# Attention over full 64-row tiles, with a short path chosen by a bound of all scores, and two key chunks per group

## The chip, the cores and the metric

The kernel runs on one core of one Trainium2 chip. A core has a matrix engine (TensorE, PE in the profile, with its weight loads shown as PEld), a vector engine (VectorE, DVE), a scalar engine (ScalarE, ACT), a general engine (GpSimd, POOL) and an engine that only issues transfers here (SyncE, SP). The metric is the time of one execution on the device in microseconds, from the first instruction to the last. Lower is better.

## The reference

The kernel computes one transformer block with adaptive layer norm, on x of shape (2, 2048, 576), with 16 heads of 36 features, everything in 32-bit floats. Cut to what matters:

```python
mod = silu(c) @ w_ada + b_ada                # six vectors of 576 per image
xn  = ln(x, 1e-6) * (1 + sc_msa) + sh_msa
q, k, v = split(xn @ w_qkv + b_qkv)          # (2, 2048, 16, 36) each
q = ln(q, 1e-5, qn_g, qn_b)                  # per head, over its 36 features
k = ln(k, 1e-5, kn_g, kn_b)
attn = softmax(einsum('bqhd,bkhd->bhqk', q, k) * 36 ** -0.5)
o = einsum('bhqk,bkhd->bqhd', attn, v) @ w_proj + b_proj
x = x + g_msa * o
h = gelu(modulated_ln(x) @ w1 + b1)          # 576 -> 2304
return x + g_mlp * (h @ w2 + b2)
```

In the inputs the gains qn_g and kn_g are ones, and the biases qn_b and kn_b are zeros.

## The kernel before

The work runs in stages: the modulation vectors (lines 121 to 181); then for each of the two images the attention inputs (L220), attention (L289) and the projection (L423); then the feed-forward part over blocks of 512 rows (L468 on). A framework turns the program into one instruction list for each engine. It keeps the written order as a priority, but an instruction that isn't ready can be passed by later ones. An engine executes its list in order, and waits where an operand or a buffer isn't there. SyncE's list holds nearly all loads, in the written order; the loads of the attention weights (L225 to L227) are written after the modulation stage and don't depend on it.

Attention works on pairs of heads. A pair's two heads of 36 features are padded to 64 rows each, so that one fills partitions 0 to 63 and the other 64 to 127. `prepare` takes one block of 512 rows of q or k: GpSimd copies it into a padded `stage` tile whose remaining rows are zero, four TensorE transposes turn it by features into the one bank `tp`, and VectorE moves it into `kt` or `qt` with gain and bias. Eight such blocks make a pair (four of k, four of q).

The softmax needs two rounds. In the first, `largest` multiplies q by k with one tile of 128 queries against 512 keys, for both heads, on 36 rows each (L338), and VectorE takes the largest score of each query (L345). `shifted_q` then puts the negated maximum into the 37th feature of a fresh copy of q (the `stage_m` tiles), against a row of ones in k, so that the second round gives shifted scores. In the second round `scores` takes a chunk of 128 keys against a block of 512 queries, on 37 rows (L360), and ScalarE applies the exponential (L364). `values` multiplies the result by v on all 128 rows, with 64 output columns for each head (L370), and accumulates over the 16 key chunks in the one bank `acc`. A 37th column of ones in v gives the sum of the softmax. `finish` copies `acc` to SBUF on ScalarE (L380), transposes it back (L383), and VectorE divides (L386, L388).

The loop at L402 goes over 8 pairs and 64 steps (4 query blocks of 16 key chunks). A step issues the scores of one chunk, a max step of the next pair, and the values of the chunk before. The first pair's max round stands alone ahead of the loop (L398), and the last pair has no max round beside it. Every matmul in 32-bit floats is two instructions. PSUM holds three double banks for scores and maxima (`s`), one `acc` and one `tp`.

## Time and profile before

| | |
|---|---|
| median of 3 runs | 6044.8 us (6020.16 to 6089.19) |
| the profiled execution | 6044.47 us |
| its span | 6042.7 us, 47052 instructions |
| mean granted TensorE clock | 0.878 of full speed |
| TensorE busy | 5862.5 us (97%) |
| VectorE, ScalarE, GpSimd busy | 1873.6, 1441.3, 288.1 us |
| chain of work that ended last | scores L360 21%, values L370 20%, max round L338 19%, feed-forward L507 10%, attention inputs L244 9% |

The profile is one execution on the chip. The clock is the share of full speed that the chip granted to TensorE; the profile gives it for each of 40 slices, or for any stretch. A busy time of TensorE is the time in which at least one matmul was under way, so two that run side by side count once. A group row gives the line, engine, operation and operands, the count, the busy time, the mean of one in ns, and the idle time before them with what ended it. A timeline row gives the start and the length in us of neighbouring instructions of one kind; the distance from one start to the next shows what a part really costs, since the ends are modelled.

### The profile page before, as it was taken

Reading aid. Unit: us, or ns where it says so; the run is one execution under the profiler, and the core shown is the slowest. Engines: PE = TensorE matmul, PEld = TensorE weight load, DVE = VectorE, ACT = ScalarE, POOL = GpSimd, SP = SyncE. Lnnn points to the kernel's source line nnn. Section 1 sums busy time; section 2 is a strip of 40 time slices with the busy share of each in tenths; the row PEclk is TensorE's granted clock in tenths of the full one; section 3 lists DMA queues with packets and bytes.
Section 4 is the critical chain, followed back from the end, with each engine's and each line's share of the span. In section 5 each row is a group of like instructions: output and inputs, shape, how many; then the busy total and the mean of one; then the engine's idle time right before and its main releaser. Section 6 shows DMA issues by size and latency. Waiting matters only on the chain.

```text
span 6042.7 us, 47052 instructions
## 1 busy us (share of the span) xinstructions
PE 5862.5 (97%) x20336; PEld 2405.9 (40%) x20336; DVE 1873.6 (31%) x2128; ACT 1441.3 (24%) x1789; POOL 288.1 (5%) x388
## 2 busy tenths in 40 slices
PE   8999999999999998999999999999999699999999
PEld 5643323332323325653233323233223355555555
DVE  3453433443433312445343334334321100000000
ACT  1101322332322342110232323223233111111110
POOL 0110000000000002110000000000001100000000
PEclk9965977997978899985898879779799899999999
DMA  3000000000000004000000000000001300000000
GB/s 107 10 1 0 1 1 0 0 1 1 1 0 1 1 1 128 12 0 0 0 1 0 1 0 0 0 0 1 0 1 50 119 16 16 16 16 16 16 8 8
DMA packets 35392, 83.60 MB, mean 14 GB/s; under 512 B 4832, under 2 KB 4832, under 8 KB 35184
## 3 DMA queue, kind: packets, MB, share of 16 engines
q1 hardware_dynamic: 29936, 61.69, 3.3%
q0 software_dynamic: 5248, 18.90, 0.8%
q8 instruction: 159, 2.61, 0.2%
q14 instruction: 49, 0.40, 0.0%
HBM read 61.68 MB, written 18.89 MB: 13 GB/s over the span
## 4 chain that ended last, share of the span: by engine, by line
PE 92%; issue 4%; DMA 1%; DVE 1%; SPq 0%; POOL 0%; ACT 0%; POOLq 0%; DVEq 0%; ACTq 0%
PE s L360 21%; PE acc L370 20%; PE s L338 19%; PE s L507 10%; PE s L244 9%; PE s L521 7%; PE s L445 3%; PE tp L313 2%; PE tp L204 1%; PE tp L383 1%; PE tp L133 0%; DMA x<-x_dram 0%; DVE qs L316 0%; DMA xt<-in_x_dram 0%; DMA wa<-in_w_ada_dram 0%
## 5 line engine op out<-in xcount | busy, mean ns | idle before, releaser
L345 DVE TENSOR_REDUCE mx<-s 128x2 f32<-128x1024 f32 x1024 | 1255.7, 1226 | 1987.9 <-PE s L338 1987.9
L364 ACT ACTIVATE pt<-s 128x1024 f32<-128x1024 f32 x1024 | 1047.7, 1023 | 2299.6 <-PE s L360 2299.5
L360 PE MATMUL s<-qs,kt 37*128 37x512 f32 x4096 | 1332.6, 732 | 14.5 <-DVE qs L316 14.5
L338 PE MATMUL s<-kt,qt 36*128 36x512 f32 x4096 | 1310.4, 735 | 0.0
L370 PE MATMUL acc<-pt,vt 128*64 128x512 f32 x4096 | 1274.6, 705 | 0.7 <-ACT pt L364 0.7
L338 PEld LDWEIGHTS s<-kt,qt 36*128 36x128 f32 x4096 | 489.2, 232 | 651.2 <-issue 648.9
L360 PEld LDWEIGHTS s<-qs,kt 37*128 37x128 f32 x4096 | 349.6, 208 | 893.5 <-issue 559.8
L507 PE MATMUL s<-xnt,w_sb 128*128 128x512 f32 (+1 forms) x1440 | 676.5, 614 | 0.3 <-ACT xnt L212 0.3
L370 PEld LDWEIGHTS acc<-pt,vt 128*64 128x64 f32 x4096 | 221.6, 148 | 878.6 <-issue 868.7
L521 PE MATMUL s<-w_sb,ht 128*128 128x288 f32 x2304 | 563.9, 407 | 0.0
L244 PE MATMUL s<-wq,xnt 128*128 128x288 f32 (+1 forms) x1920 | 542.8, 427 | 8.1 <-DMA wq<-in_w_qkv_dram 7.7
L521 PEld LDWEIGHTS s<-w_sb,ht 128*128 128x128 f32 x2304 | 436.6, 191 | 118.1 <-issue 1.5
L244 PEld LDWEIGHTS s<-wq,xnt 128*128 128x128 f32 (+1 forms) x1920 | 334.9, 190 | 206.2 <-issue 143.0
L507 PEld LDWEIGHTS s<-xnt,w_sb 128*128 128x128 f32 (+1 forms) x1440 | 248.1, 189 | 420.3 <-issue 387.0
L514 ACT ACTIVATE ht<-s,b_sb 128x512 f32<-128x512 f32 x144 | 98.9, 687 | 949.6 <-PE s L507 949.4
L529 DVE TENSOR_TENSOR y<-s,gate 128x576 f32<-128x576 f32 x32 | 24.2, 758 | 604.5 <-PE s L521 604.5
L445 PE MATMUL s<-wp,ott 128*128 128x288 f32 (+1 forms) x640 | 181.3, 426 | 2.2 <-DMA wp<-in_w_proj_dram 2.2
L197 DVE TENSOR_SCALAR xn<-x,mv,rstd 128x576 f32<-128x576 f32 x32 | 18.6, 585 | 491.6 <-PE acc L205 491.1
L308 POOL COPY stage_m<-qk 128x288 f32<-128x288 f32 x64 | 27.2, 427 | 2740.0 <-PE tp L313 2740.0
L445 PEld LDWEIGHTS s<-wp,ott 128*128 128x128 f32 (+1 forms) x640 | 112.1, 191 | 62.5 <-issue 39.6
L316 DVE TENSOR_SCALAR qs<-tp,gain_q,bias_q 128x512 f32<-128x512 f32 x64 | 51.8, 810 | 238.4 <-PE tp L313 238.4
L272 ACT ACTIVATE sq<-qk 128x1152 f32<-128x1152 f32 x32 | 37.2, 1162 | 326.5 <-DVE qk L268 326.5
(84 smaller groups left out, 1636.1 us busy)
## 6 DMA issues: line engine op xcount, KB each, us to landing
xt<-in_x_dram SPq DMA_DIRECT2D x64, 288.0 KB
x_dram<-x POOLq DMA_DIRECT2D x32, 288.0 KB, 3.5
x<-x_dram SPq DMA_DIRECT2D x8, 1152.0 KB
out_dram<-y POOLq DMA_DIRECT2D x32, 288.0 KB, 2.4
wa<-in_w_ada_dram SPq DMA_DIRECT2D x6, 1152.0 KB
wq<-in_w_qkv_dram SPq DMA_DIRECT2D x6, 1152.0 KB
w_sb<-in_w_dram SPq DMA_DIRECT2D x3, 1728.0 KB
w_sb<-in_w_dram SPq DMA_DIRECT2D x4, 1152.0 KB
```

The lines of the kernel that those rows point to most:

```text
L204: nc.tensor.transpose(t4[:, k * P : (k + 1) * P], src[:, k * P : (k + 1) * P], ident)
L244: nc.tensor.matmul(ps[:, a, :HALF], xnt[:kk, k, :], wq[:kk, k, f0 : f0 + HALF], start=(k == 0), stop=(k == NKC - 1),)
L313: nc.tensor.transpose(tp[:, i * P : (i + 1) * P], st[:, i].rearrange("p h e -> p (h e)"), ident)
L338: nc.tensor.matmul(ps[:, h, :], qts[p, blk][r, i * P : (i + 1) * P], kts[p][r, kq * BLK : (kq + 1) * BLK], start=True, stop=True,)
L345: nc.vector.tensor_reduce(maxima[p, blk][:, i, :, kq], ps, AX.X, ALU.max)
L360: nc.tensor.matmul(ps[:, h, :], kts[p][r, kc * P : (kc + 1) * P], qt[r, :], start=True, stop=True)
L364: nc.scalar.activation(pt, ps, AF.Exp, scale=SCALE)
L370: nc.tensor.matmul(acc[64 * h : 64 * h + 64, :], vt[:, v0 : v0 + 64], pt[:, h, :], start=(kc == 0), stop=(kc == NT - 1),)
L445: nc.tensor.matmul(ps[:, a, :HALF], ott[:kk, k, :], wp[:kk, k, a * HALF : (a + 1) * HALF], start=(k == 0), stop=(k == NKC - 1),)
L507: nc.tensor.matmul(ps[:, j, :], w1_sb[:kk, k, f * P : (f + 1) * P], xnt[:kk, k, :], start=(k == 0), stop=(k == NKC - 1),)
L514: nc.scalar.activation(ht[:, f, :], ps[:, j, :], AF.Gelu, bias=b1_sb[:, f : f + 1])
L521: nc.tensor.matmul(ps[:, a, :HALF], ht[:, f, i * P : (i + 1) * P], w2_sb[:, f, a * HALF : (a + 1) * HALF], start=(f == 0), stop=(f == NF - 1),
```

## The change

The kernel now computes a bound on all scores before the stages: after the norm, a head's q and k have at most the length that the largest gain and the largest bias allow. If the bound is at most 32, a flag is 1. All engines read the flag after the modulation stage and branch: on 1, every image's attention takes the new `attention_of_small`, on 0 the old `attention`. Attention inputs, projection and the feed-forward part stand in both branches, unchanged. The PSUM pools are opened once for the modulation stage and again in each branch.

`attention_of_small` has no max round and no shifted q, and applies the exponential to the plain scores. Scores use all 64 rows of a head's tile, of which 28 are zero. A group covers two key chunks: scores of both, then possibly the finish of a query block and a prepare of the next pair, then the values of the group before. Groups run on across pairs without a drain. The copy of `acc` is on VectorE, and the transposes of `finish` come one group later. There are four `pt` buffers instead of three, and k and q of a pair are one tile each. The old path's matmuls of both rounds are also set to 64 rows.

```diff
+    gb = const.tile([1, 2, 2, HD], F32, name="gb")
+    for i, (g_in, b_in) in enumerate(((qn_g, qn_b), (kn_g, kn_b))):
+        nc.scalar.dma_start(out=gb[:, i, 0, :], in_=g_in.unsqueeze(0))
+        nc.scalar.dma_start(out=gb[:, i, 1, :], in_=b_in.unsqueeze(0))
+    neg = const.tile([1, 2, 2, HD], F32, name="neg")
+    nc.vector.tensor_scalar_mul(neg, gb, -1.0)
+    nc.vector.tensor_tensor(neg, neg, gb, ALU.max)
+    most = const.tile([1, 2, 2], F32, name="most")
+    nc.vector.tensor_reduce(most, neg, AX.X, ALU.max)
+    length = const.tile([1, 2], F32, name="length")
+    nc.vector.tensor_reduce(length, most, AX.X, ALU.add)
+    product = const.tile([1, 1], F32, name="product")
+    nc.vector.tensor_tensor(product, length[:, 0:1], length[:, 1:2], ALU.mult)
+    small_sb = const.tile([1, 1], I32, name="small_sb")
+    nc.vector.tensor_scalar(small_sb, product, BOUND / (HD * SCALE), None, ALU.is_le)
...
+    def attention_of_small(b, qk, vt):
...
+            def scores(p, qb, kc):
+                ps = s_tile()
+                for h in range(2):
+                    r = slice(64 * h, 64 * h + 64)
+                    nc.tensor.matmul(
+                        ps[:, h, :],
+                        kts[p][r, kc * P : (kc + 1) * P],
+                        qts[p][r, qb * BLK : (qb + 1) * BLK],
+                        start=True,
+                        stop=True,
+                    )
+                pt = b2p.tile([P, 2, BLK], F32, name="pt", bufs=4)
+                nc.scalar.activation(pt, ps, AF.Exp, scale=SCALE)
+                return pt
...
+            for i in range(2 * NBLK):
+                prepare(0, i)
+            groups = [(p, qb, kc) for p in range(NPAIR) for qb in range(NBLK) for kc in range(0, NT, 2)]
+            per_pair = NBLK * NT // 2
+            behind, done = None, None
+            for g, (p, qb, kc) in enumerate([*groups, (None, None, None)]):
+                pts = None if p is None else [scores(p, qb, kc), scores(p, qb, kc + 1)]
+                if done is not None:
+                    finish(*done)
+                    done = None
+                i, at = divmod(g % per_pair, 3)
+                if p is not None and p + 1 < NPAIR and at == 2 and i < 2 * NBLK:
+                    prepare(p + 1, i)
+                if behind is not None:
+                    bp, bqb, bkc, bpts = behind
+                    if bkc == 0:
+                        acc = acc_tile()
+                    for i in range(2):
+                        values(bp, acc, bpts[i], bkc + i)
+                    if bkc == NT - 2:
+                        ot = b2p.tile([P, BLK], F32, name="ot")
+                        nc.vector.tensor_copy(ot, acc)
+                        done = (bp, bqb, ot)
+                behind = (p, qb, kc, pts)
+            finish(*done)
...
     def attention(b, qk, vt):
...
-                    r = slice(64 * h, 64 * h + HD)
+                    r = slice(64 * h, 64 * h + 64)
...
-                    r = slice(64 * h, 64 * h + HV)
+                    r = slice(64 * h, 64 * h + 64)
...
+    def block(small):
+        with tc.tile_pool(name="qkv", bufs=1) as qkvp:
+            for b in range(B):
...
+                attention_inputs(b, qk, vt, vv)
+                (attention_of_small if small else attention)(b, qk, vt)
+                projection(b, qk)
...
+    is_small = nc.values_load(small_sb[0:1, 0:1], min_val=0, max_val=1)
+    with tc.If(is_small > 0) as branch:
+        with psum_pools():
+            block(True)
+    with branch.Else():
+        with psum_pools():
+            block(False)
```

`prepare`, `values` and `finish` of the new function are those of the old one, but for the tiles and the copy named above.

## The prediction

> **What bounds the kernel now.** I read the groups of instructions first, then stretches with their granted clock, then single steps on the timeline. In the group rows the columns are busy time, mean ns of one, and idle time before.

> ```profile
> PE 5862.5 (97%) x20336; PEld 2405.9 (40%) x20336; DVE 1873.6 (31%) x2128; ACT 1441.3 (24%) x1789; POOL 288.1 (5%) x388
> ...
> PEclk9965977997978899985898879779799899999999
> ```

> ```profile
> L360 PE MATMUL s<-qs,kt 37*128 37x512 f32 x4096 | 1332.6, 732 | 14.5 <-DVE qs L316 14.5
> L338 PE MATMUL s<-kt,qt 36*128 36x512 f32 x4096 | 1310.4, 735 | 0.0
> L370 PE MATMUL acc<-pt,vt 128*64 128x512 f32 x4096 | 1274.6, 705 | 0.7 <-ACT pt L364 0.7
> L345 DVE TENSOR_REDUCE mx<-s 128x2 f32<-128x1024 f32 x1024 | 1255.7, 1226 | 1987.9 <-PE s L338 1987.9
> L364 ACT ACTIVATE pt<-s 128x1024 f32<-128x1024 f32 x1024 | 1047.7, 1023 | 2299.6 <-PE s L360 2299.5
> ...
> L380 ACT COPY ot<-acc 128x512 f32<-128x512 f32 x64 | 37.5, 585 | 176.1 <-PE acc L370 176.1
> ```

> TensorE is busy for 97% of the span; VectorE (L345) and ScalarE (L364) wait for it. Three groups of equal size fill attention: scores (L360), the max round (L338), values (L370). The clock row falls in attention, the middle of each half. The next rows are stretches: start and end, length, PE busy with its instructions, granted clock.

> ```profile
> 382.00:486.00 104.00, 104.00 (x246) 0.50 0.00 0
> ...
> 2160.00:2280.00 120.00, 120.00 (x476) 1.00 0.00 1
> ```

> ```profile
> 362.64:2286.16 1923.52, 1891.05 (x6652) 0.83 0.00 1
> 2692.00:4620.69 1928.69, 1896.50 (x6653) 0.82 0.00 1
> ```

> The first is the max round alone (L338): PE is never idle, yet at half clock throughout. The second is the last head pair, which has no max round: full clock. The last two rows are the attention of image 0 and of image 1, from the first transpose to the last. With a clock of either 0.5 or 1, a mean of 0.83 puts 34% of image 0's time at half clock, and 0.82 puts 36% of image 1's there.

> Single steps (one key chunk: scores, max, values, four matmuls each) show both speeds. First a step at full clock, then one at half, then the end of a half-clock spell:

> ```profile
> 2138.47 1.13 PE L360 MATMUL s<-qs,kt 37*128 37x512 f32 x4
> 2139.43 1.03 PE L338 MATMUL s<-kt,qt 36*128 36x512 f32 x4
> 2140.38 1.08 PE L370 MATMUL acc<-pt,vt 128*64 128x512 f32 x4
> 2141.39 1.13 PE L360 MATMUL s<-qs,kt 37*128 37x512 f32 x4
> ```

> ```profile
> 1002.24 2.08 PE L360 MATMUL s<-qs,kt 37*128 37x512 f32 x4
> 1004.11 1.92 PE L338 MATMUL s<-kt,qt 36*128 36x512 f32 x4
> 1005.96 1.98 PE L370 MATMUL acc<-pt,vt 128*64 128x512 f32 x4
> ```

> ```profile
> 832.04 1.98 PE L370 MATMUL acc<-pt,vt 128*64 128x512 f32 x4
> 833.95 1.12 PE L313 MATMUL tp<-ident,stage_m 128*128 128x128 f32 x4
> 835.00 1.90 PE L370 MATMUL acc<-pt,vt 128*64 128x512 f32 x4
> 836.82 1.13 PE L360 MATMUL s<-qs,kt 37*128 37x512 f32 x4
> ```

> A full-clock step takes 2141.39 - 2138.47 = 2.92 us (0.96 scores, 0.95 max, 1.01 values). At half clock the scores take 1.87 and the max 1.85, the values 833.95 - 832.04 = 1.91: 5.63. The last block shows how a spell ends: values, transposes and values, all on 128 rows, run for 4.8 us without a 36- or 37-row matmul between, and the scores after them take 1.13 again. My reading: the gate opens on a few us in which most array rows work; matmuls on 36 or 37 rows, two at a time, leave it shut, but do not shut it once open if values stand between them.

> [...]

> **The change, part by part, as a new attention stage.** I build it from TensorE's rows, since nothing else is near: per group of two chunks ScalarE has 2 x 1.02 = 2.05 us of exponentials.

> ```profile
> 4606.27 1.13 PE L360 MATMUL s<-qs,kt 37*128 37x512 f32 x4
> 4607.33 1.08 PE L370 MATMUL acc<-pt,vt 128*64 128x512 f32 x4
> 4608.34 1.13 PE L360 MATMUL s<-qs,kt 37*128 37x512 f32 x4
> ```

> ```profile
> 2143.31 1.94 PE L370 MATMUL acc<-pt,vt 128*64 128x512 f32 x8
> ...
> 2149.08 1.99 PE L360 MATMUL s<-qs,kt 37*128 37x512 f32 x8 [0.91 <-DVE qs L316]
> ```

> *Max round out, two chunks per group.* The last pair already runs scores and values alone: 1.06 + 1.01 = 2.07 us per chunk. Doubling four matmuls to eight of one kind adds 1.94 - 1.08 = 0.86 (values) and 1.99 - 1.13 = 0.86 (scores), so of 2.07 some 0.35 is the change from one kind to the other. A group of two chunks costs 1.06 + 0.86 + 1.01 + 0.86 = 3.79 us. Per image: 8 pairs x 4 query blocks x 8 groups = 256 groups, 970.2 us.

> *64 rows for 37.* No row shows a 64-row score. Bounds: at the price of the 37-row one above (columns streamed are the same 512), or cheaper by the change of kind, 0.35 per group, if that came from odd rows. The values, on all 128 rows, take as long as the scores, so I take no gain. The new rows hold zeros. If the gate counts rows by instruction, the loop opens it within one group; if it counts data, the first prepare's transposes between values do it as in the 832 us rows, after two or three groups. A half-clock group costs 1.87 + 1.69 + 1.91 + 1.72 = 7.19 (1.69 is the 104 us over 246/4 steps, 1.72 twice 0.86), 3.4 more; one to three of them, I take 3.4 us.

> ```profile
> 983.41 0.66 PE L313 MATMUL tp<-ident,stage_q 128*128 128x128 f32 x4
> 984.00 1.08 PE L370 MATMUL acc<-pt,vt 128*64 128x512 f32 x4
> ```

> ```profile
> 364.82 1.09 PE L313 MATMUL tp<-ident,stage_k 128*128 128x128 f32 x4 [1.07 <-POOL stage_k L308]
> 366.91 1.09 PE L313 MATMUL tp<-ident,stage_k 128*128 128x128 f32 x4 [1.00 <-DVE kt L316]
> ```

> *Transposes.* One block of four takes 984.00 - 983.41 = 0.59 us among matmuls. Per image 7 x 8 = 56 prepares, 33.0, and 31 finishes within the loop, 18.3. The first 8 prepares run as before, one per 366.91 - 364.82 = 2.09: 16.7. The 32 of the shifted query go, with their waits at pair ends; so does the drain there, since groups now run on across pairs.

> *Finish.* The copy of the accumulator moves to VectorE: 0.59 us as on ScalarE, or 0.61, half of L345's 1.23. It runs under the next group's 1.92 us of scores; without that cover it would add up to 0.6 x 32 = 19 us per image. The finish of one group and a prepare fall together once per pair and share one tp bank: VectorE's reciprocal and multiply then hold the transposes up to 1.0 us (the idle times in the last rows), 0 to 7 per image; I take 3. The last copy and transposes add 1.5.

> Sum per image: 970.2 + 33.0 + 18.3 + 16.7 + 3.4 + 3 + 1.5 = 1046. Saved: 1923.5 - 1046 = 877 and 1928.7 - 1046 = 883, together 1760. Of that the clock is 0.34 x 1923.5/2 + 0.36 x 1928.7/2 = 674; removed work is the rest.

> *Bound and branch.* Four small loads on ScalarE's queue and seven tiny VectorE operations come before the first Silu and the first modulation, where both engines otherwise wait for loads and matmuls: nothing; uncovered, four issues of 0.36 us (the first row below) on ScalarE, 1.4. The branch is new, and stands ahead of the loads of the attention weights. What is queued behind it is everything:

> ```profile
> 50.92 0.36 SPq L225 DMA_DIRECT2D bq<-in_b_qkv_dram  x1
> ...
> 69.58 0.52 POOL L171 DMA_DIRECT2D gate_dram<-gb  x1 [0.26 <-DVE gb L169]
> ```

> ```profile
> q8 instruction: 159, 2.61, 0.2%
> ```

> Today SyncE issues those loads from 50.92, under the modulation stage. If the engines pass the branch one by one, the cost is a register read and the fetch of a far instruction block; the instruction queue's row (packets, MB, share of 16 engines' span) gives 0.002 x 16 x 6043/159 = about 1.2 us per packet, so some 3 us, twice with the way out. If all must first be done, the loads start after 69.58: 19 us later, 25 in all. No gain is possible, as nothing starts earlier. I take 12.

> [...]

> The profiled execution took 6044.5 us (span 6042.7), the median 6044.8, so no correction: 6044.5 - 1760 + 12 = 4296.

> **Rivals.** *Half clock all through.* If zero rows count as idle and nothing opens the gate, an image costs 256 x 7.19 + 87 x 1.05 + 21 = 1953 (1.05 is 835.00 - 833.95), that is 30 and 24 us more than now: 6044.5 + 54 + 12 = 6111, slower by 1.1%. It becomes a loss only when over 96% of attention is at half clock. Against it: the last pair at 1.00, already half 37-row work, and two chunks of values running 3.6 us together. 3%.

> *Groups broken up.* If the order written is not kept and scores and values alternate chunk by chunk, each step costs 2.07: 512 x 0.35 = 179 more, 4475. The order of the transposes at 833.95, ahead of the block's last values, shows that the order follows readiness; three score banks against two in use speak against it. 6%.

> *Spells of half clock remain.* At today's share of the time, about 35%, an image would take 1046/(1 - 0.35/2) = 1268, 222 more: 4740 at most; a few spells, less. Spells now start in the idle time at pair ends, which goes. 7%.

> *The other branch.* With gains of one and biases of zero the product is 1, under 32/(36/6) = 5.3, so the short path is taken. Were it not, only the 64 rows would act: at best 6044.5 - 674 + 12 = 5383. 2%.

> **The numbers.** The forecast has 82%: 4296. Its own ends are 4230 (a cheaper change of kind for part of the groups) and about 4350 (branch 25, copies uncovered 38). The range reaches to the broken groups and short spells: 4235 to 4480. A measurement of this kernel can tell about 1%; faster by more has 95%, within 1% 2% (a gate that opens only now and then), slower 3%.

> **What would show it.** Right: a granted clock near 1.00 over attention; groups of eight score matmuls and eight values every 3.8 us; attention of 1045 us per image; no reduces of 1226 ns; the first attention load a few to 20 us later than 50.92. Wrong: clocks of 0.5 beyond the first groups, four-by-four alternation, or PE idle on exponentials or on the accumulator's copy.

## The result, and the profile after

The changed kernel takes 4282.3 us (median; single runs 4281.93 to 4282.63), against 6052.4 for the kernel before in the same comparison. The ratio is 0.7074, 95% interval 0.7033 to 0.7115: 29% faster. The forecast was 4296. The profiled execution took 4281.93 us with a span of 4279.9; before it was 6044.47.

From the page and the groups of the changed kernel (scores are now L361, values L375, exponentials L369, the copy of the accumulator L419, the transposes of `finish` L386):

```profile
PE 4154.1 (97%) x15984; PEld 1916.8 (45%) x15984; DVE 609.2 (14%) x1046; ACT 1348.8 (32%) x1725; POOL 258.5 (6%) x316
...
PEclk8999999999999999999999999998899999999999
```

```profile
L361 PE MATMUL s<-qt,kt 64*128 64x512 f32 x4096 | 1021.4, 617 | 0.0
L375 PE MATMUL acc<-pt,vt 128*64 128x512 f32 x4096 | 1006.6, 605 | 0.0
L369 ACT ACTIVATE pt<-s 128x1024 f32<-128x1024 f32 x1024 | 992.6, 1021 | 1056.3 <-PE s L361 1056.2
...
L419 DVE COPY ot<-acc 128x512 f32<-128x512 f32 x64 | 44.3, 692 | 806.9 <-PE acc L375 806.9
...
L386 PE MATMUL tp<-ident,ot 128*128 128x128 f32 x256 | 42.0, 287 | 1.6 <-DVE ot L419 1.6
```

TensorE is still the bound, 97% busy, with 15984 matmul instructions instead of 20336. The max round's group is gone, and so are VectorE's reduces (its busy time fell from 1873.6 to 609.2 us). The scores fell from 1332.6 to 1021.4 us and the values from 1274.6 to 1006.6, with as many matmuls over as many columns. Two things make this up: the clock row has no low slices in attention any more, and eight matmuls of a kind in a row take less than twice four (1.99 us below, against twice the 1.13 of four in the old last pair). The run with one chunk per group, below, parts them: an estimate from its rows at full clock, 1024 x 1.13 and 1024 x 1.08 us, gives 1157 and 1106, so about 176 and 169 us are the clock and the rest is the longer groups. The attention of the two images, first transpose to last, as stretches with PE busy and granted clock:

```profile
362.86:1404.98 1042.12, 1036.45 (x4477) 0.99 0.00 1
1812.10:2854.93 1042.83, 1037.17 (x4476) 0.99 0.00 1
```

It was 1923.5 and 1928.7 us at a clock of 0.83 and 0.82. The two differences, 881.4 and 885.9, are 1767 us; the whole execution gained 6044.47 - 4281.93 = 1763. So outside attention about 4 us were lost. Two groups in the middle, on the timeline of TensorE:

```profile
803.07 1.99 PE L361 MATMUL s<-qt,kt 64*128 64x512 f32 x8
804.99 1.94 PE L375 MATMUL acc<-pt,vt 128*64 128x512 f32 x8
806.85 1.99 PE L361 MATMUL s<-qt,kt 64*128 64x512 f32 x8
808.77 0.66 PE L350 MATMUL tp<-ident,stage_k 128*128 128x128 f32 x4
809.36 1.94 PE L375 MATMUL acc<-pt,vt 128*64 128x512 f32 x8
```

A group takes 806.85 - 803.07 = 3.78 us, and a prepare's transposes 809.36 - 808.77 = 0.59 more.

### The profile page after: what moved, and what is told of

Its sections match the earlier page's. It is cut to its first block, busy times and chain, and to the rows that moved or that the text cites. A ratio compares the mean times of both kernels' runs of the same rounds, so it can differ in the third digit from the quotient of the medians.

```text
span 4279.9 us, 37104 instructions
## 1 busy us (share of the span) xinstructions
PE 4154.1 (97%) x15984; PEld 1916.8 (45%) x15984; DVE 609.2 (14%) x1046; ACT 1348.8 (32%) x1725; POOL 258.5 (6%) x316
## 3 DMA queue, kind: packets, MB, share of 16 engines
q8 instruction: 127, 2.08, 0.2%
## 4 chain that ended last, share of the span: by engine, by line
PE 91%; issue 5%; DMA 2%; DVE 1%; SPq 1%; POOL 0%; ACT 0%; DVEq 0%; POOLq 0%; ACTq 0%
PE s L361 23%; PE acc L375 23%; PE s L643 14%; PE s L279 12%; PE s L657 10%; PE s L580 4%; PE tp L350 2%; PE tp L239 1%; PE tp L386 1%; PE tp L168 1%; DMA x<-x_dram 0%; DMA xt<-in_x_dram 0%; DMA wa<-in_w_ada_dram 0%; DMA wp<-in_w_proj_dram 0%; DMA w_sb<-in_w_dram 0%
## 5 line engine op out<-in xcount | busy, mean ns | idle before, releaser
L369 ACT ACTIVATE pt<-s 128x1024 f32<-128x1024 f32 x1024 | 992.6, 1021 | 1056.3 <-PE s L361 1056.2
L361 PE MATMUL s<-qt,kt 64*128 64x512 f32 x4096 | 1021.4, 617 | 0.0
L375 PE MATMUL acc<-pt,vt 128*64 128x512 f32 x4096 | 1006.6, 605 | 0.0
L361 PEld LDWEIGHTS s<-qt,kt 64*128 64x128 f32 x4096 | 353.7, 186 | 653.5 <-issue 462.1
L375 PEld LDWEIGHTS acc<-pt,vt 128*64 128x64 f32 x4096 | 251.5, 136 | 587.7 <-issue 482.0
L419 DVE COPY ot<-acc 128x512 f32<-128x512 f32 x64 | 44.3, 692 | 806.9 <-PE acc L375 806.9
L353 DVE TENSOR_SCALAR qt<-tp,gain_q,bias_q 128x512 f32<-128x512 f32 x64 | 51.8, 810 | 491.1 <-PE tp L350 491.1
L353 DVE TENSOR_SCALAR kt<-tp,gain_k,bias_k 128x512 f32<-128x512 f32 x64 | 51.8, 810 | 487.9 <-PE tp L350 487.9
L247 ACT ACTIVATE xnt<-tp,mod 128x128 f32<-128x128 f32 x256 | 99.1, 456 | 56.0 <-PE tp L239 55.6
L239 PE MATMUL tp<-ident,xn 128*128 128x128 f32 x256 | 45.2, 303 | 63.8 <-DVE xn L232 46.9
L313 POOL TENSOR_TENSOR qk<-qk,inv 128x1152 f32<-128x1152 f32 x32 | 71.5, 2234 | 479.1 <-DVE inv L312 479.1
```

The costliest lines, as they stand in the source:

```text
L239: nc.tensor.transpose(t4[:, k * P : (k + 1) * P], src[:, k * P : (k + 1) * P], ident)
L247: nc.scalar.activation(dst[:m, k, :], t4[:, k * P : (k + 1) * P] if k < 4 else t1[:64, :P], AF.Identity, bias=mod[:m, which, k, b : b + 1] ...
L353: nc.vector.tensor_scalar(to[p][:, blk * BLK : (blk + 1) * BLK], tp, gains[n], biases[n], ALU.mult, ALU.add)
L361: nc.tensor.matmul(ps[:, h, :], kts[p][r, kc * P : (kc + 1) * P], qts[p][r, qb * BLK : (qb + 1) * BLK], start=True, stop=True,)
L369: nc.scalar.activation(pt, ps, AF.Exp, scale=SCALE)
L375: nc.tensor.matmul(acc[64 * h : 64 * h + 64, :], vt[:, v0 : v0 + 64], pt[:, h, :], start=(kc == 0), stop=(kc == NT - 1),)
```

## The experiments

They stand in the order in which they take the change apart. Times are medians. The runs come from several comparisons, in which the kernel before had medians of 6041 to 6068 us, so differences of a few us are read from the traces as well.

**What the max round alone is worth.** It is taken out of the kernel before; the shift of the softmax is then zero, as in the changed kernel, and all else of the old loop stays.

```diff
-            for s in range(steps):
-                largest(0, s)
...
-                nc.vector.tensor_reduce(
-                    st[:, :, :, HD], maxima.pop((p, qb)), AX.X, ALU.max, negate=True
-                )
...
-                    if p + 1 < NPAIR:
-                        largest(p + 1, s)
```

> The kernel before with the max round taken out and nothing else: no largest, the shift stays zero, the copies and transposes of the shifted q, the 37 rows, single chunks and the drain at pair ends stay. Theory (the max round alone is most of the gain): per image 8 x (64 x 2.07 + 4.5 of drain) + 32 x (0.59 + 0.59) + 56 x 0.59 + 16.7 = 1184 us at full clock, so 6044.5 - (1923.5 + 1928.7 - 2 x 1184) = 4560 us; if the drains shut the gate and 37 rows keep it shut for a query block, each costs 16 x 1.7 = 27 us, up to 4830 us. Rival (two chunks and 64 rows carry the gain): above 5300 us.

Measured: 4862 us, a little over the upper end. The max round is 1190 of the 1770 us. The clock was 0.909 over the span and 0.85 in image 0's attention. What happens at the end of each pair, on TensorE's timeline (scores are L357, values L367):

```profile
554.58 1.08 PE L367 MATMUL acc<-pt,vt 128*64 128x512 f32 x4
556.34 0.66 PE L380 MATMUL tp<-ident,ot 128*128 128x128 f32 x4 [0.69 <-ACT ot L377]
557.95 0.63 PE L313 MATMUL tp<-ident,stage_m 128*128 128x128 f32 x4 [0.95 <-DVE qk L385]
559.48 3.16 PE L357 MATMUL s<-qs,kt 37*128 37x512 f32 x8 [0.90 <-DVE qs L316]
562.57 1.98 PE L367 MATMUL acc<-pt,vt 128*64 128x512 f32 x4
564.48 2.08 PE L357 MATMUL s<-qs,kt 37*128 37x512 f32 x4
```

The drain leaves TensorE idle three times within 4 us (the times in brackets), and from 561 on it runs at half speed (a score step of four takes 2.08 instead of 1.13), for 24 to 61 us. All seven pair ends of image 0 show such a spell. Some end with the transposes at a query block's end, as in the prediction's rows; others, this one too, end in the middle of plain alternation:

```profile
582.14 1.98 PE L367 MATMUL acc<-pt,vt 128*64 128x512 f32 x4
584.04 1.13 PE L357 MATMUL s<-qs,kt 37*128 37x512 f32 x4
```

So in this trace the clock came back to full in the midst of 37-row scores alternating with values too, only late: 23.9 us at half.

**The same with the scores on 64 rows.** The 27 added rows are zero.

```diff
-                    r = slice(64 * h, 64 * h + HV)
+                    r = slice(64 * h, 64 * h + 64)
```

> The kernel before without its max round, now with the scores on 64 rows; drains, shifted q and single chunks stay. Theory (rows decide how soon the gate opens again after the idle time at a pair's end): the half-clock spells of up to 60 us after each pair shrink to a few us, and the time falls from 4862 to the full-clock sum, 4560 us. Rival (the spells have another cause than the 37 rows): 4800 us or more.

Measured: 4572 us, 290 less, as the theory says. The same place in this kernel:

```profile
692.62 0.63 PE L313 MATMUL tp<-ident,stage_m 128*128 128x128 f32 x4 [0.95 <-DVE qk L385]
694.15 3.68 PE L357 MATMUL s<-qs,kt 64*128 64x512 f32 x8 [0.91 <-DVE qs L316]
697.76 1.08 PE L367 MATMUL acc<-pt,vt 128*64 128x512 f32 x4
```

The clock falls here too (eight score matmuls take 3.68 us instead of 1.99), and is full again by the values behind them (four take 1.08); 3.4 us were at half.

**The 64 rows in the old kernel with its max round.** Both rounds on 64 rows, nothing else.

```diff
-                    r = slice(64 * h, 64 * h + HD)
+                    r = slice(64 * h, 64 * h + 64)
...
-                    r = slice(64 * h, 64 * h + HV)
+                    r = slice(64 * h, 64 * h + 64)
```

> The kernel before, both rounds kept, with the max and score matmuls on 64 rows instead of 36 and 37; the added rows are zero in q or k. Theory (the gate counts rows by instruction, zeros too): the pure max round runs at full clock and spells at half clock vanish but for a few us after idle time at pair ends, 6044.5 - 674 = 5370 us. Rival (the gate looks at the data, or row width is no matter): 6045 us.

Measured: 5478 us, ratio 0.9054 (0.9008 to 0.9101). The theory holds, but its price was 108 us too good against the 6044.5 it started from (84 against the 6068 of its own comparison). Its stretches, the pure max round and then the attention of image 0:

```profile
382.00:446.00 64.00, 63.30 (x228) 1.00 0.00 1
363.20:2006.21 1643.01, 1608.28 (x6652) 0.98 0.00 1
```

The pure max round is at full clock, and attention is at 0.98. It saved 280 us per image, not the 327 that halving all half-clock time gives. In the pure max round 64 us now hold 228/4 = 57 steps, 1.12 us each instead of 0.85 (half of 1.69). VectorE holds it: it starts a reduce every 1.13 us, ten in 11.39 us of which the last takes 1.23, and TensorE still counts as busy:

```profile
381.64 11.39 DVE L345 TENSOR_REDUCE mx<-s 128x2 f32<-128x1024 f32 x10
```

In the loop a step falls from 5.63 to 2.92, not to 2.82, and the waits at pair ends are as long as before: 14.5 us in all for the shifted query (L316), 13.4 for VectorE's result (L388) and 11.0 for the copy (L380), the same in both traces.

**How many rows it takes.** The same kernel with both rounds on 48 and on 42 rows.

```diff
-                    r = slice(64 * h, 64 * h + HD)
+                    r = slice(64 * h, 64 * h + 48)
...
-                    r = slice(64 * h, 64 * h + HV)
+                    r = slice(64 * h, 64 * h + 48)
```

> The kernel before with both rounds on 48 rows, 75% of the array's rows for a pair of matmuls, where 36 are 56% and 64 all. Theory (the gate weighs working rows against a threshold above 75%): the pure max round stays at 0.50, and spells in the loop end earlier or not, 5478 to 6050 us. Rival (any tile over half full counts as full above some row count between 36 and 48): the pure max round at 1.00 and about 5480 us.

> The kernel before with both rounds on 42 rows, 66% of the array's rows for a pair of matmuls; 36 leave the gate shut in the pure max round and 48 (75%) open it. Theory (a threshold on rows, about 70%, without a reason for the figure): at 0.50 in the pure max round and near 6000 us if the threshold lies above 66%, about 5490 us if below. Rival (a gradual effect): in between, near 5750 us.

Measured: 5491 us with 48 rows, and 5657 (one run) with 42. The pure max round, first with 48, then with 42:

```profile
382.00:446.00 64.00, 63.32 (x222) 0.95 0.00 1
```

```profile
382.00:446.00 64.00, 64.00 (x152) 0.50 0.00 0
```

So in the pure round the clock was 0.95 on 48 rows and 0.50 on 42. The theory's claim that 48 rows are too few falls. Yet 42 rows aren't 36: in the loop the two half-clock spells between 700 and 1200 us last 20.5 and 34.2 us, where those of the kernel before last 85 to 89, and the time lies between, as the rival had it. The first of the two, in pieces of 5 us:

```profile
715.00:720.00 5.00, 4.09 (x12) 0.60 0.00 0
720.00:725.00 5.00, 5.00 (x12) 0.50 0.00 0
725.00:730.00 5.00, 5.00 (x14) 0.50 0.00 0
730.00:735.00 5.00, 5.00 (x12) 0.50 0.01 2
735.00:740.00 5.00, 5.00 (x20) 0.85 0.01 3
```

At half clock are 4.0, 15 and 1.5 us, together 20.5. In the same way the spells after image 0's pair ends last 85.3 to 88.8 us in the kernel before, and 23.9 to 61.4 in the run without the max round. An estimate of the mean rows at work weighs them by the half-clock times above, 1.69 us for four score or max matmuls and 1.72 for four values, and divides by the step. Of the 128 rows of the values the old loop's step of 5.63 us then has 65% at work, the step with 42 rows 70%, and scores and values alone (3.91 us, from 564.48 to 568.39 above) 69%. Spells are longest with the first, 85 to 89 us, against 20 to 61 with the other two. Whether that share is what decides, no run tests.

**The short path with 36 rows.** All else as changed.

```diff
             def scores(p, qb, kc):
...
-                    r = slice(64 * h, 64 * h + 64)
+                    r = slice(64 * h, 64 * h + HD)
```

> The short path with its scores on 36 rows again instead of 64, all else as changed. Theory (row width decides only when the clock gate opens; values between the scores hold it open): the loop starts at half clock and opens at the first prepare between values, one to three groups of 3.4 us late per image, so 4285 to 4305 us. Rival (64 rows keep the gate open all along): spells of half clock return, 4700 us at today's share of 35%, up to 6100 us if it never opens.

Measured: 4287.5 us, 5 more than with 64. Only the start differs. The start of image 0's attention, first in the changed kernel, then with 36 rows:

```profile
374.27 2.08 PE L361 MATMUL s<-qt,kt 64*128 64x512 f32 x4
376.28 1.11 PE L350 MATMUL tp<-ident,stage_q 128*128 128x128 f32 x4
377.32 1.33 PE L361 MATMUL s<-qt,kt 64*128 64x512 f32 x4
378.58 0.66 PE L350 MATMUL tp<-ident,stage_q 128*128 128x128 f32 x4
```

```profile
384.36 3.68 PE L375 MATMUL acc<-pt,vt 128*64 128x512 f32 x8
387.97 2.29 PE L361 MATMUL s<-qt,kt 36*128 36x512 f32 x8
390.19 0.66 PE L350 MATMUL tp<-ident,stage_k 128*128 128x128 f32 x4
```

With 64 rows the second score step is already nearly at speed (1.33 instead of 2.08). With 36 the clock is full only behind the first block of values, ahead of the first prepare that the theory named, at about 388.6, 11 us later. After that neither loses the clock in attention: the one with 64 rows is at 1.00 from 385 to 1400.

**One chunk per group.** Here on 64 rows, and then on 36.

```diff
-            groups = [(p, qb, kc) for p in range(NPAIR) for qb in range(NBLK) for kc in range(0, NT, 2)]
-            per_pair = NBLK * NT // 2
+            groups = [(p, qb, kc) for p in range(NPAIR) for qb in range(NBLK) for kc in range(NT)]
+            per_pair = NBLK * NT
...
-                pts = None if p is None else [scores(p, qb, kc), scores(p, qb, kc + 1)]
+                pts = None if p is None else [scores(p, qb, kc)]
...
-                i, at = divmod(g % per_pair, 3)
+                i, at = divmod(g % per_pair, 6)
...
```

> The changed kernel with one key chunk per group instead of two. Theory (0.35 us per change between scores and values and back, paid twice as often): 512 x 0.35 = 179 us more, 4461 us, groups of 2.07 us at full clock. Rival (the change of kind was a matter of 37 rows, or hidden): under 4300 us.

> The changed kernel with one chunk per group and scores on 36 rows, that is, without both of its additions to the short path, but still without drains and shifted q. Theory (no idle time, so the open gate is held): 4446 us as with one chunk on 64 rows, plus 5 to 25 us for a later opening, 4450 to 4470 us. Rival (alternating single chunks on 36 rows lose the clock): 4700 us or more.

Measured: 4446 us on 64 rows (164 more than with two chunks), 4453 on 36. Steps on 64 rows:

```profile
801.75 1.13 PE L361 MATMUL s<-qt,kt 64*128 64x512 f32 x4
802.81 1.08 PE L375 MATMUL acc<-pt,vt 128*64 128x512 f32 x4
803.82 1.13 PE L361 MATMUL s<-qt,kt 64*128 64x512 f32 x4
```

A step is 2.07 us, to the digit that of the old last pair on 37 rows: the change of kind cost the same there as here. Image 0's attention is 83 us longer, not 256 x 0.35 = 90. Part of that is at the ends: single chunks bring the first values 2 us earlier and leave one block of values instead of two behind the last scores. Single chunks on 36 rows don't lose the clock either (1.00 from 400 to 700), so grouping isn't what holds the clock up here.

**Four chunks per group.** Six buffers for the exponentials' results, and one prepare per group from the fourth group of a pair.

```diff
-            groups = [(p, qb, kc) for p in range(NPAIR) for qb in range(NBLK) for kc in range(0, NT, 2)]
-            per_pair = NBLK * NT // 2
+            groups = [(p, qb, kc) for p in range(NPAIR) for qb in range(NBLK) for kc in range(0, NT, 4)]
+            per_pair = NBLK * NT // 4
...
-                pts = None if p is None else [scores(p, qb, kc), scores(p, qb, kc + 1)]
+                pts = None if p is None else [scores(p, qb, kc + j) for j in range(4)]
...
-                i, at = divmod(g % per_pair, 3)
-                if p is not None and p + 1 < NPAIR and at == 2 and i < 2 * NBLK:
+                i, at = g % per_pair - 3, 2
+                if p is not None and p + 1 < NPAIR and at == 2 and 0 <= i < 2 * NBLK:
...
-                pt = b2p.tile([P, 2, BLK], F32, name="pt", bufs=4)
+                pt = b2p.tile([P, 2, BLK], F32, name="pt", bufs=6)
...
```

> The changed kernel with four key chunks per group, six buffers for the exponentials' results instead of four, and prepares one per group from the fourth group of a pair. Theory (one change of kind, 0.35 us, per four chunks instead of per two): 256 of 512 changes go, 90 us, 4193 us, groups of 7.24 us. Rival (three score banks and the exponentials' buffers hold the matmuls up): 4282 us or more, with waits of the scores on ScalarE.

Measured: 4203.6 us, 79 less than the changed kernel and the fastest of all. The columns are as above:

```profile
801.60 3.71 PE L361 MATMUL s<-qt,kt 64*128 64x512 f32 x16
805.24 0.66 PE L350 MATMUL tp<-ident,stage_q 128*128 128x128 f32 x4
805.82 3.65 PE L375 MATMUL acc<-pt,vt 128*64 128x512 f32 x16
809.40 3.70 PE L361 MATMUL s<-qt,kt 64*128 64x512 f32 x16
```

Four chunks take 7.80 us with a block of transposes, 7.22 without: no stall on the three score banks. ScalarE now often waits for a buffer that the values free (543 us in all), which costs TensorE nothing: its scores and values have 0.0 us of idle time before them.

**The branch.** The changed kernel without flag load and branch, the short path alone.

```diff
-    is_small = nc.values_load(small_sb[0:1, 0:1], min_val=0, max_val=1)
-    with tc.If(is_small > 0) as branch:
-        with psum_pools():
-            block(True)
-    with branch.Else():
-        with psum_pools():
-            block(False)
+    with psum_pools():
+        block(True)
```

> The changed kernel without the flag's load and the branch: the short path alone, the bound still computed. Theory (engines pass the branch one by one, no barrier; the trace shows the first transposes 0.6 us later than before): 4278 to 4282 us. Rival (a barrier and fetches on the way in and out): 12 to 25 us less, 4257 to 4270 us.

Measured: 4280.1 us, 2 less, with single runs from 4277.7 to 4282.2 that reach into those of the changed kernel. The first load and the first transpose of the attention inputs, in the changed kernel and then without the branch:

```profile
52.15 0.36 SPq L260 DMA_DIRECT2D bq<-in_b_qkv_dram  x1
...
75.44 1.08 PE L239 MATMUL tp<-ident,xn 128*128 128x128 f32 x4 [8.27 <-DVE rstd L230]
```

```profile
50.88 0.41 SPq L260 DMA_DIRECT2D bq<-in_b_qkv_dram  x1
...
74.80 1.08 PE L239 MATMUL tp<-ident,xn 128*128 128x128 f32 x4 [7.94 <-DVE rstd L230]
```

SyncE passes the branch and issues 1.3 us later, but long before the modulation stage issues its last transfer at 69.03, so there is no barrier. TensorE starts 0.6 us later, which says little: without the branch the first transpose of image 0's attention comes at 362.64 us in the kernel before and at 363.99 in the run on 42 rows, and at 362.86 in the changed kernel. The way out shows behind the last output's issue, here again first with the branch and then without:

```profile
4270.86 0.54 POOL L668 DMA_DIRECT2D out_dram<-y  x1 [16.92 <-DVE y L666]
```

```profile
4272.53 0.54 POOL L668 DMA_DIRECT2D out_dram<-y  x1 [16.92 <-DVE y L666]
```

The spans end at 4279.9 and 4279.5, that is 9.0 and 7.0 us later. In the kernel before, without a branch, this tail is 6.9 us (issue at 6035.76, span 6042.7). So the branch costs about 2.1 us, nearly all of it on the way out.

## Why the prediction was right, and where it wasn't

*The group.* 3.79 us was forecast from rows of the old last pair, 3.78 came. Its parts hold as well: 0.86 for four more matmuls of the same kind, 0.35 for the change of kind and back. The runs with one, two and four chunks per group (4446, 4282, 4204) pay that price 1024, 512 and 256 times: 164 and 79 us for what 0.35 makes 179 and 90, so 0.32 and 0.31 a time over the whole kernel. Between max round and scores the old step pays no such price: both use 36 or 37 rows for each head, on different operands, and the max round added only 2.92 - 2.07 = 0.85 us, as four more matmuls of the same kind do. What it is that costs 0.35 us between scores and values, no trace shows.

*Attention.* Forecast 1046 us per image, measured 1042.1 and 1042.8. The transposes took 0.59 as forecast. The 3 us for a finish and a prepare that share one bank don't show: in the seven groups of image 0 that hold both, the prepare's transposes went out behind six of the eight values, and TensorE has no idle time from the first scores to the last values. The copy on VectorE took 0.69 us instead of 0.61, with 1.6 us of waiting in all (L386 above): the 1.9 us of scores cover it.

*The gate.* So the prediction calls what takes the granted clock from 0.50 to 1.00. Its reading of the old rows held in these runs. Opening: with 64 rows the clock was full 3.5 us after the first scores at 374.27, and about 5 us after them in image 1, though the added rows are zero; in a pure max round it took 48 rows about 7 us of unbroken work, and 104 us on 36 rows and 64 us on 42 stayed at 0.50. Holding: on 36 rows, with values between them, a full clock stayed full (1.00 from 400 to 700 with one chunk per group). One part was too strong: short rows between values don't always leave the clock at half, as its rise at 584 us in the run without the max round shows.

*The clock's share.* This part of the account failed, though the forecast didn't hang on it: attention was built up from full-clock rows. "Of that the clock is 674" took half of all half-clock time; 64 rows alone gave 566 (6044.5 - 5478), or 590 against their own comparison. Of the 47 us missing in image 0 (327 - 280), an estimate from the rows above gives 17 to the reduces in the pure max round (64 steps of 1.12 instead of 0.85) and about 30 to the 4% of attention that a clock of 0.98 puts at half; within the rounding of the clocks that is all of it. And the parts don't add up: once the max round is out, 64 rows are worth 290 us, and once the drains are gone as well, 5 (7 with one chunk per group). With the max round out, either of the two nearly cures the clock by itself: with 64 rows it was back 3.4 us after a drain had taken it (at 694 and at 842 us), and without drains TensorE doesn't idle in the loop, and 36 rows stayed at 1.00. In these runs the rows matter where the clock is at half: after idle time, and in the pure max round. The order of steps that the runs show is

| from the kernel before to the changed one | us | step |
|---|---|---|
| before | 6052 | |
| max round out | 4862 | -1190 |
| scores on 64 rows | 4572 | -290 |
| rest of the short path, one chunk per group | 4446 | -126 |
| two chunks per group | 4282 | -164 |

The 126 us hold all that is left of the change: no drains, no shifted q, the copy on VectorE, a fourth `pt` buffer, the branch. They were not taken apart, and in another order the steps would have other sizes.

*The branch.* 12 us were taken, in the middle between the engines passing one by one (3, and 3 on the way out) and a barrier (25). It cost about 2.1, and the mechanism was the first: no barrier, loads 1.3 us later under cover of the modulation stage, and the rest on the way out. The value should have gone to the low end: the bounds were two mechanisms, and a middle between mechanisms is neither. Outside attention 4 us were lost in all, where 12 were forecast, and attention saved 1767 instead of 1760: together about the 14 us between 4296 and 4282. The bound's operations on VectorE are six, not seven, and cost nothing: the last starts at 4.68 us, and VectorE's next work at 23.7. That a fetch of instructions is what the 1.3 and 2.1 us pay for, as the 3 us took it, no run shows.

*The rivals.* Half clock all through and broken groups didn't come: nowhere in attention do scores and values alternate four by four. Remaining spells didn't come either, but their mechanism is real, as the run without the max round shows. The other branch wasn't taken; its price of 5383 would have been too low by some 100 us, as the old path on 64 rows shows.

## What to carry to other kernels

Before a busy TensorE is called the bound, look at its granted clock stage by stage: here a third of attention ran at half clock with TensorE busy for 1891 of its 1923.5 us. Where short contractions meet a half clock, as here, pad them to the full 64 rows with zeros (here the padded scores took no longer: 2.07 us a step with their values, as on 37 rows), and leave no idle time ahead of stages in which short-row matmuls follow (here 24 to 61 us at half clock after each pair's end). Matmuls of one kind belong together in runs as long as the banks allow; that price, here 0.35 us, is read off the old trace, and halving the number of changes saved 164 and then 79 us.

## What the runs showed of the hardware that was not expected

The kernel before varies far more than the others: its single runs spread from 5941 to 6103 us, those of the changed kernel from 4281.9 to 4282.6. It would fit that the same drain lowers the clock at some pair ends and not at others (in the trace of before the clock stayed at 1.00 over the drain at 1227 us, and the one at 985 was followed by 88.7 us at half), so that a run's time depends on how often. This was not tested.

The branch between two whole paths of over 4000 us each, taken by all engines, cost about 2 us here, with the flag ready long before (at 4.8 us), and nearly all of it lay behind the last output (9.0 us instead of 7.0).
